# Gated cross-attention plus top-2 expert layer on one core: a reordered front, fixed PSUM banks, work moved between engines, tail blocks with both expert layers

## The chip, the core and the metric

The kernel runs on one core of a Trainium2 chip. The metric is device time in microseconds (us) from launch to end, the median of several runs. Engines are named as in the profile: PE is the matrix engine (PEld its weight loads), DVE the VectorE, ACT the ScalarE, POOL the GpSimd engine, SP the engine that issues most DMAs. All arithmetic is fp32, except some routing matrices of zeros and small whole numbers, which are bf16.

## What is computed

```python
xn  = layernorm(x)                                   # x: 4 x 256 x 256
q, k = ctx @ Wq.T + bq, ctx @ Wk.T + bk              # ctx: 4 x 256 x 128
att = softmax(q @ k.T)                               # 256 x 256 for each of 4 batches
x   = x + tanh(g_xattn) * (xn @ att.T)
t   = layernorm(x)                                   # 1024 rows
probs = softmax(gelu(t @ rw1) @ rw2)                 # 8 experts
w, idx = top_k(probs, 2)
for e in 8 experts, k in 2 choices:                  # I = 1024
    Y = gelu(t @ w1[e] + b1[e]) @ w2[e] + b2[e]      # rows whose k-th choice is e
    C = gelu(b1[e]) @ w2[e] + b2[e]                  # all the other rows, if any row chose e
    out += w[k] * where(idx[k] == e, Y, C)
x = x + tanh(g_ffn) * out
```

The constant C of an expert needs the product of gelu(b1[e]) with w2[e]. A row of an expert's hidden layer has gelu(b1[e]) subtracted, so that the constant can be added to all rows at the end.

## The kernel before

**Front.** Rows are held in 8 tiles of 128 (two for each batch). One string, `order` (L446), lists every step of attention, second layernorm and gating; each step puts its instructions on fixed engines, and every engine works through its own instructions in the order in which the string names them. Step names used below, with the key of a batch or a group of tiles behind a colon: `qk` the two projections on PE (L218), `q` and `k` their evictions with bias (L225, L228), `en` the scores on PE, `nmax` the negated row maximum on DVE (L243), `exp` on ACT, `rden` the reciprocal of the sum (L258), `norm` the scaling (L264: DVE, for batch 3 ACT), `pt` and `attT` transposition and eviction, `st`, `pw`, `xn` the first layernorm (statistics on DVE, power -0.5 on POOL, scaling on DVE, for batch 3 POOL), `tra` and `xnT` its transposition, `po` the product with the attention, `add` the residual on DVE (L350), `sf`, `pf`, `xf` the second layernorm (`xf` also writes the rows to DRAM through SP), `trf`, `xT`, `r`, `gel`, `lg` the gate network, `chosen` (L396) the ranks of the eight logits on DVE, `gb1` the gelu of all b1, `table:F` a one-element activation that loads F's table, `w2:n` n loads of 1 MB of w2 through SP. PSUM tiles come from a pool of eight banks in turn. Batch 3 stays behind: its `po`, `add` and gate are done later.

**Routing.** Rows of the first six tiles (12 groups of 128 row-choices) are sorted into slots of 128 rows, each of one expert (L930): `cnt`, `pc`, `scan`, `over`, `runs`, `past`, `who`, `lead`, `rank`, `pos`, `split`, `put` are small DVE and PE steps, `hq_` (L647) makes a 128x128 one-hot matrix for each group on DVE, `inv_` (L651) multiplies them on PE, and `lists` writes the row numbers. `fill:0` loads w1 of slot 0 through SP as soon as `who` is known; `gather` (L760, POOL) fetches a slot's rows from DRAM.

**Slots.** Each slot has `turn` (L773: two PE transposes of the gathered rows, an ACT copy), `first_layer` (L787: 8 x 2 matmuls `h`, a gelu on ACT for each 128 hidden units, two subtractions on DVE) and `second_layer` (L809: 8 matmuls `y` of 128x256, scaling `ys` on DVE, an indirect DMA from POOL that adds the rows to the output, each after the one before). The fixed loop (L1013) has 16 slots and always runs `first_layer(s)` and then `second_layer(s - 1)`. Two queues of small work, `main` and `second`, are slipped in between the matmuls by a credit in us (`between`, L998). `main` holds what batch 3 still needs (`xf:3`, `r:3`), the sorting of the remaining rows, and then the constants: for each expert eight DVE steps `bias_path` (L838), two `both_`, and at the end one DMA that adds the constants to the output (L888).

**Between routing and slot 1** the order is written out (L930 to L942): `gather:0`, `gather:1`, `table:Gelu`, `turn(0)`, then ACT copies the expert list (`who_later`), on which SP waits before it can load w1 of slot 1; five DMAs `ow` bring the rows x to the output, and `sf:3 pf:3` run ahead of `gather:4` (slots 2 to 4).

**Tail.** How many slots are used is known only at run time: blocks of `tc.If` follow (L1046). A block runs `first_layer(s)` and `second_layer(s - 1)`; when no slot follows, an Else runs the last `second_layer`.

## Time and profile before

| what | value |
|---|---|
| median of 3 runs | 203.71 us (203.51 to 204.03) |
| the profiled execution | 202.87 us |
| its span, first to last instruction | 201.1 us |
| PE busy | 178.9 us (89%), 1198 matmul records |
| DVE, ACT, POOL busy | 134.7, 88.1, 73.1 us |
| slots that ran | 19 (L796 has 608 records, 32 for a slot) |
| one slot in the middle (turn, h, y) | 0.22 + 3.57 + 3.46 = 7.25 us |

An fp32 matmul leaves two records. In the timeline the durations of neighbours on one engine overlap a little, so the distance between two starts is what an instruction occupies. The page's row PEclk is the granted clock of PE, in tenths of full speed; before the first clock record (10.9 us into the span) it says nothing.

### The profile page before, as it was taken

What the parts mean: (1) busy time and instruction counts of PE and PEld (TensorE: products, weight loads), DVE (VectorE), ACT (ScalarE), POOL (GpSimd) and SP (SyncE); (2) the same over time, 40 slices, a digit from 0 to 9 for tenths busy, and PEclk for the clock granted to TensorE, in tenths of its full rate; (3) what the DMA queues carried; (4) which work ended last, traced back from release to release, by engine and by line L of the source; (5) the groups of instructions that cost most, each with busy time, mean ns of one, the idle gap of its engine ahead of it and who ended that gap; (6) DMA issues with size and microseconds to landing.
All of it is one profiled execution on the core that took longest, in us unless ns stands there. A gap on an engine that the chain in (4) does not pass through costs nothing.

```text
span 201.1 us, 3845 instructions
## 1 busy us (share of the span) xinstructions
PE 178.9 (89%) x1198; PEld 159.3 (79%) x1198; DVE 134.7 (67%) x401; ACT 88.1 (44%) x234; POOL 73.1 (36%) x89
## 2 busy tenths in 40 slices
PE   3999885389799999999999999999999999999930
PEld 1677573359599899998999999999899989999820
DVE  2879988875558969889689999999756222222200
ACT  2275455434554262362463364265196255255000
POOL 5314510046107146341614522522535504646130
PEclk9999999756999999999999999999999999999995
DMA  6799969945996994317478668699713493423121
GB/s 182 225 335 351 348 194 293 367 170 154 344 414 267 256 404 107 52 14 221 78 241 246 217 234 256 186 401 332 220 39 52 53 172 42 64 39 51 39 31 21
DMA packets 23688, 38.76 MB, mean 193 GB/s; under 512 B 2440, under 2 KB 17808, under 8 KB 23664
## 3 DMA queue, kind: packets, MB, share of 16 engines
q1 hardware_dynamic: 18208, 32.16, 46.6%
q0 software_dynamic: 4880, 6.17, 17.9%
q8 instruction: 13, 0.21, 0.5%
q10 hardware_dynamic: 576, 0.13, 0.3%
q14 instruction: 11, 0.09, 0.1%
HBM read 33.21 MB, written 5.64 MB: 193 GB/s over the span
## 4 chain that ended last, share of the span: by engine, by line
PE 65%; DMA 14%; DVE 11%; issue 6%; POOL 1%; ACT 1%; SPq 0%; POOLq 0%; ACTq 0%; DVEq 0%
PE h L796 27%; PE y L815 26%; DMA out<-ys,give 8%; DMA xg<-rows,take 3%; PE qk L223 2%; DMA ctx_sb<-in_ctxT 2%; PE po L339 2%; PE xt L780 2%; DVE acc L353 1%; DVE nmax L246 1%; DVE att L272 1%; DVE st_f L292 1%; PE r L381 1%; PE inv L655 1%; POOL out L820 1%
## 5 line engine op out<-in xcount | busy, mean ns | idle before, releaser
L796 PE MATMUL h<-xs,w 128*128 128x128 f32 x608 | 74.1, 279 | 0.5 <-ACT xs L781 0.5
L796 PEld LDWEIGHTS h<-xs,w 128*128 128x128 f32 x608 | 71.4, 195 | 1.0 <-ACT xs L781 0.9
L815 PE MATMUL y<-w_all,hT 128*128 x304 | 69.5, 381 | 0.1
L800 ACT ACTIVATE hT<-h,bsel 128x128 f32<-128x128 f32 x152 | 55.5, 368 | 14.9 <-PE h L796 4.2
L815 PEld LDWEIGHTS y<-w_all,hT 128*128 128x128 f32 x304 | 56.1, 190 | 7.2 <-issue 0.3
L803 DVE TENSOR_TENSOR hT<-hT,gbsel 128x512 f32<-128x512 f32 x38 | 26.2, 690 | 25.1 <-ACT hT L800 25.0
L820 POOL DMA_INDIRECT out<-ys,give x14 | 22.5, 1609 | 54.3 <-DVE ys L818 32.1
L781 ACT COPY xs<-xt 128x256 f32<-128x256 f32 x20 | 7.5, 372 | 61.7 <-PE xt L780 61.7
L765 POOL DMA_INDIRECT xg<-rows,take x23 | 25.0, 1085 | 22.7 <-ACT prob L695 15.0
L842 DVE SCALAR_TENSOR_TENSOR gsum<-w_all,gb,gsum 128x256 f32<-128x256 f32 x56 | 27.1, 483 | 1.5
L818 DVE TENSOR_SCALAR ys<-y,share 128x256 f32<-128x256 f32 x19 | 9.1, 481 | 16.7 <-PE y L815 16.6
L820 POOL DMA_INDIRECT out<-ys,take x5 | 8.5, 1710 | 16.8 <-DVE ys L818 10.3
L780 PE MATMUL xt<-ident,xg 128*128 128x128 f32 x40 | 8.0, 283 | 2.0 <-ACT xT L374 0.9
L780 PEld LDWEIGHTS xt<-ident,xg 128*128 128x128 f32 x40 | 5.4, 144 | 5.3 <-PE po L339 1.2
L339 PE MATMUL po<-attT,xnT 128*128 128x256 f32 x24 | 7.8, 479 | 0.0
L299 POOL TENSOR_TENSOR rstd_a<-rstd_a,halves 128x2 f32<-128x2 f32 x4 | 3.0, 750 | 12.0 <-DVE rden L260 7.0
L280 PE MATMUL pt<-ident,att 128*128 128x128 f32 x16 | 3.2, 327 | 4.2 <-ACT att L268 4.0
L223 PE MATMUL qk<-ctx_sb,wq_sb 128*128 128x256 f32 x6 | 3.5, 686 | 3.8 <-DMA wq_sb<-in_wqT 3.4
L697 POOL TENSOR_TENSOR prob<-euler,prob 128x16 f32<-128x16 f32 x1 | 2.9, 2932 | 10.5 <-DVE capped L586 10.5
L851 DVE SCALAR_TENSOR_TENSOR both<-gsum,act,both 128x256 f32<-128x256 f32 x14 | 6.4, 481 | 0.2
L339 PEld LDWEIGHTS po<-attT,xnT 128*128 128x128 f32 x24 | 5.4, 236 | 1.2 <-ACT attT L285 0.3
L280 PEld LDWEIGHTS pt<-ident,att 128*128 128x128 f32 x16 | 1.9, 156 | 5.5 <-ACT att L268 4.4
(201 smaller groups left out, 172.3 us busy)
## 6 DMA issues: line engine op xcount, KB each, us to landing
w<-in_w SPq DMA_DIRECT2D x18, 1024.0 KB
w_all<-in_w SPq DMA_DIRECT2D x8, 1024.0 KB
acc<-in_x SPq DMA_DIRECT2D x4, 256.0 KB
w<-in_w SPq DMA_DIRECT2D x2, 512.0 KB
out<-acc POOLq DMA_DIRECT2D x1, 1024.0 KB
rows<-xf SPq DMA_DIRECT2D x3, 256.0 KB
out<-acc SPq DMA_DIRECT2D x3, 256.0 KB
ctx_sb<-in_ctxT SPq DMA_DIRECT2D x3, 128.0 KB
```

What stands on the lines that cost most here:

```text
L223: nc.tensor.matmul(dst, lhsT=w, rhs=ctx3 if b == "3" else ctx_sb[:, int(b), :], start=True, stop=True)
L339: nc.tensor.matmul(ps[:, ts(i, N)], lhsT=live["xnT", b][:, n, ts(t % LT, P)], rhs=live["attT", b][:, n, :], start=(n == 0), stop=(n == NN ...
L765: nc.gpsimd.indirect_dma_start(out=xg, out_offset=None, in_=rows[0 : EARLY * P if s < NA else T, :], in_offset=bass.IndirectOffsetOnAxis(a ...
L780: nc.tensor.transpose(ps[:, ts(c, P)], xg[:, ts(c, P)], ident)
L781: nc.scalar.copy(xs, ps[:, 0:D].rearrange("p (c l) -> p c l", c=DC))
L796: nc.tensor.matmul(ps[:, 0:P], lhsT=w1_sb[:, c, ts(ch, P)], rhs=xs[:, c, :], start=(c == 0), stop=(c == DC - 1),)
L800: nc.scalar.activation(hT[:, ch, :], ps[:, 0:P], AF.Gelu, bias=bias[:, ch : ch + 1])
L803: nc.vector.tensor_tensor(hT[:, part, :], hT[:, part, :], gbias[:, part].rearrange("p (i o) -> p i o", o=1).to_broadcast([P, 4, P]), ALU.s ...
L815: nc.tensor.matmul(ps[:, 0:D], lhsT=hT[:, i, :], rhs=w2_sb[:, i, :], start=(i == 0), stop=(i == IC - 1))
L818: nc.vector.tensor_scalar(ys, ps[:, 0:D], go.share[:, j : j + 1], None, ALU.mult)
L820: nc.gpsimd.indirect_dma_start(out=total[0:last_row, :], out_offset=bass.IndirectOffsetOnAxis(ap=go.give[:, j : j + 1], axis=0), in_=ys, i ...
L842: nc.vector.scalar_tensor_tensor(gsums[e], w2_all[:, e, c, :], gb1[:, e, c : c + 1], b2_row[e % 2] if c == 0 else gsums[e], ALU.mult, ALU.add)
```

## The change

- **PSUM**: eight fixed banks, each step's bank written in a table (`bank_of`); the pools of the slot phase open after routing.
- **Loads**: the four context tiles are loaded ahead of the four x tiles. Of w2, five loads as before, two after `xf:2a`, one behind `fill:0`.
- **PE at the start**: seven matmuls of a constant tile (`ahead:7`).
- **Attention by query halves** for batches 0 and 2 (keys x and y). `norm` moves to ACT for batches 1 to 3, `xn` of batch 1 to POOL, the epsilon of both layernorms from DVE to POOL. The gate factor tg moves from `norm` into `add`, which becomes a scalar_tensor_tensor. Tiles 2 and 3 become groups 1a and 1b. Logits of batches 0 and 1 are copied by ACT, and tiles 4 and 5 are ranked together.
- **Routing**: of the 12 one-hot matrices DVE makes 8, POOL 2 (`hqp`), ACT 2 (`hqa`, a Square and a Relu for each); `put` comes behind them, `po:3` behind `inv`.
- **Constants of experts 0 and 1** on PE: 16 matmuls `ce` with one column of gelu(b1) as the stationary operand, placed between routing steps, and two ACT copies `cec`; 14 net `bias_path` steps on DVE fall away.
- `sf:3 pf:3` run before `turn(0)`. The `ow` DMAs are four.
- **Tail**: `second_layer(15)` follows the fixed loop, and each block runs `first_layer(s)` and then `second_layer(s)`; there is no Else. The first three blocks are not nested.

```diff
+    banks = [psum.tile([P, 512], F32, name=f"bank{i}") for i in range(8)]
...
-    load_x(0)
-    nc.sync.dma_start(out=ctx_sb[:, 1, :], in_=ctxT[:, 1, :])
-    load_x(1)
...
+    nc.sync.dma_start(out=ctx_sb[:, 1 : B - 1, :], in_=ctxT[:, 1 : B - 1, :])
     nc.sync.dma_start(out=ctx3, in_=ctxT[:, B - 1, :])
-    load_x(3)
+    for b in range(B):
+        load_x(b)
...
+            if key[0] == "0":
+                nc.vector.tensor_scalar(att[:, i, :], att[:, i, :], scale, None, ALU.mult)
+            else:
+                nc.scalar.activation(att[:, i, :], att[:, i, :], AF.Copy, scale=scale)
...
-        nc.vector.tensor_scalar(rstd, mv[:, :, 1], EPS, None, ALU.add)
...
+        nc.gpsimd.tensor_scalar(rstd, mv[:, :, 1], EPS, None, ALU.add)
         nc.gpsimd.tensor_tensor(rstd, rstd, halves.to_broadcast(list(rstd.shape)), ALU.pow)
...
+        normal("a", b, rows_of(b), made("xn", b, [P, LT, D], 3), nc.gpsimd if b in "13" else nc.vector)
...
+    def ahead_(n):
+        for _ in range(int(n)):
+            nc.tensor.matmul(banks[0][:, 0:P], lhsT=ones, rhs=ones, start=True, stop=True)
+    def ce(i):
+        e, c = divmod(int(i), IC)
+        nc.tensor.matmul(
+            banks[bank_of[f"ce{e}"]][0:1, 0:D], lhsT=gb1[:, e, c : c + 1], rhs=w2_all[:, e, c, :],
+            start=(c == 0), stop=(c == IC - 1),
+        )
+    def cec(e):
+        nc.scalar.copy(sums[0:1, int(e), :], banks[bank_of[f"ce{e}"]][0:1, 0:D])
...
+        ahead:7 table:Tanh g ident w2:5 qk:0 qk:1 k:0 q:0 st:0 en:0y tg en:0x q:1 nmax:0y qk:3 pw:0 k:1 nmax:0x exp:0y
+        st:1 qk:2 k:3 exp:0x en:1 xn:0 pw:1 k:2 rden:0y q:3 rden:0x tra:0 norm:0y xn:1 q:2 nmax:1 en:3 xnT:0 norm:0x
+        masks pt:0y exp:1 st:2 en:2x pt:0x en:2y attT:0y nmax:2x pw:2 tra:1 attT:0x rden:1 st:3 po:0 norm:1 nmax:2y
+        xnT:1 xn:2 pw:3 exp:2x pt:1 nmax:3 exp:2y tra:2 xn:3 rden:2x attT:1 add:0 norm:2x po:1b rden:2y sf:0 norm:2y
+        po:1a add:1b pt:2y sf:1b pt:2x xnT:2 pf:0 tra:3 add:1a attT:2y sf:1a attT:2x pf:1b gb1 po:2b xf:0 pf:1a xf:1b
+        trf:0 xnT:3 add:2b po:2a xf:1a xT:0 sf:2b trf:1b r:0 add:2a pf:2b sf:2a xT:1b trf:1a r:1b xf:2b gel:0 pf:2a
+        xT:1a trf:2b lg:0 gel:1b xf:2a w2:2 xT:2b r:1a lc:0 trf:2a r:2b gel:1a chosen:0 xT:2a lg:1b lg:1a gel:2b r:2a
+        lc:1 ce:0 chosen:1 gel:2a lg:2b table:Exp lg:2a ce:1 chosen:2 ce:2 exp:3 ce:3
...
+        if engine is nc.scalar:
+            far = one([P, P], "far", BF16)
+            nc.scalar.activation(far, rowb, AF.Square, scale=-1.0, bias=at)
+            nc.scalar.activation(dst, far, AF.Relu, scale=-1.0, bias=ones[:, 0:1])
...
+            cnt:0 ce:4 scan pc:0 rden:3 ce:5 over:0 runs:0 norm:3 ce:6 lead:0 past:0 who:0 fill:0 w2:1 ce:7 rank:0 pt:3
+            pos:0 cec:0 ce:8 attT:3 ce:9 split:0 ce:10 hqa hqs hqp ce:11 ce:12 put:0 inv:0 po:3
+        do("lists:0 gather:0 sel:0 soft:0 gather:1")
...
+        do("ce:13 ce:14 ce:15 cec:1 wgt:0 add:3 table:Gelu sf:3 pf:3")
...
-        do("fill:1 ow:0 ow:2a ow:2b ow:1 ow:3 sf:3 pf:3 gather:4")
+        do("fill:1 ow:0 ow:1 ow:2 ow:3 gather:4")
...
+        second_layer(*pending)
...
+        with tc.If(used > s - NA):
...
             turn(s + 1, here[0])
             first_layer(s, here[1])
-            second_layer(*pending)
+            second_layer(s, here[1])
             gather(s + AHEAD)
-        with more_slots.Else():
-            with tc.If(used > s - NA - 1):
-                second_layer(*pending)
```

## The prediction

> **What bounds the kernel now.** I read the page first, its slices by engine.

> ```profile
> PE   3999885389799999999999999999999999999930
> DVE  2879988875558969889689999999756222222200
> PEclk9999999756999999999999999999999999999995
> ```

> A slice is 5.03 us. From slice 12 on PE is full: slots follow each other at 7.25 us, 14 of them without a hole. Nothing that saves DVE, ACT or POOL time can show there. What can move is when the full stretch begins (the front) and how it ends (the tail). In the front DVE is the busy engine, and PE has a hole in slices 7 and 8 that is followed by a reduced clock. The two-microsecond windows say when (columns: start:end, length, busy us and instructions of PE, PEld, DVE, ACT, POOL, granted clock, DMA share, GB/s):

> ```profile
> 36.00:38.00 2.00, 0.00 (x0) 0.00 (x0) 1.86 (x13) 0.49 (x3) 0.00 (x0) 1.00 1.09 366
> 42.00:44.00 2.00, 1.83 (x5) 0.93 (x3) 0.98 (x6) 0.65 (x2) 1.41 (x2) 0.50 0.27 86
> 46.00:48.00 2.00, 2.00 (x12) 2.00 (x11) 1.05 (x8) 0.73 (x2) 1.68 (x2) 0.50 0.29 16
> ```

> PE idles during the sort, then works at half clock from 38 to 48 us; from 42 to 48 the DMAs hardly move anything, because w1 of slot 1 has not been asked for. The chain of waits through this stretch:

> ```profile
> 39.37 0.73 PE inv L655 x24
> 40.10 3.75 PE po L339 x8
> 43.87 0.70 DVE acc L353
> ...
> 46.12 0.72 POOL rstd_f L299
> 46.85 0.19 issue
> 47.04 6.37 DMA xg<-rows,take
> 53.41 0.14 issue
> 53.55 0.41 PE xt L780 x2
> 53.95 1.45 PE h L796 x12
> ```

> So the slow `po:3` delays `add:3`, `sf:3`, `pf:3`; slot 2's gather is queued behind `pf:3` on POOL, its packets run behind w1 of slot 1, and slot 1 can't begin before 53.8. What SP waited for, and the last two scatters:

> ```profile
> SPq L894 <- ACT who_later L938: 9.0, 1, 9.0
> ```

> ```profile
> 190.23 1.56 POOL L820 DMA_INDIRECT out<-ys,give  x1 [4.04 <-DVE ys L818]
> 192.98 0.48 DVE L818 TENSOR_SCALAR ys<-y,share 128x256 f32<-128x256 f32 x1 [3.03 <-PE y L815]
> 194.85 1.55 POOL L820 DMA_INDIRECT out<-ys,give  x1 [3.05 <-DMA out<-ys,give]
> ```

> **A. Attention and gate, up to the last `chosen` (32.56 us before).** The first evictions wait for the bias load and start at 6.36; that load is unchanged, so I start the sum there. DVE's list in the new order, by distances between starts in the timeline: `k:0` 0.48; 14 tiles of statistics at 0.56, 7.9; four half maxima at 0.36 and two whole ones at 0.62, 2.7; five reciprocals 0.5; two half `norm` 0.74; ten tiles scaled by `xn` 0 and 2 and by `xf` at 0.36, 3.6; masks 0.37; `add` 0.70 plus four at 0.44 (0.02 to 0.06 over the tensor_tensor row, as L842's 0.48 stands over 0.42), 2.45; three `chosen` 1.24, 1.24, 1.43. Sum 22.6, end 29.0. Gone from DVE are eight epsilon steps (1.5), four scalings of `norm` (1.5), `xn:1` (0.7), logits copies and one split `chosen` (1.2). PE's list after 6.9 is some 20 us warm, ACT's 17.7: both end earlier, if they don't wait. Waits I find by walking the queues: `xf:2a` waits 0.6 for `pf:2a`, `chosen:0` 0.2 for ACT's copy, and I allow 0.4 for the rest. End 30.2, that is 2.4 earlier; between 1.0 (every edge late) and 3.5 (none).

> The unknown costs here: the epsilon on POOL lies between the small POOL rows (0.13) and the power itself (0.72); I take 0.2, being an add; the four or five on the path cost what the wait above holds. `xn:1` on POOL costs 2.44 (L304, two tiles) against 0.73 on DVE; `tra:1` then waits for it until about 13.4, in a queue with `po:0` behind it, but `po:0` waits for `attT:0x` until 13.9 anyway. The x loads behind the context arrive about 1 us later; DVE is held by the bias until 6.36, so this costs nothing, and up to 0.5 if they come after 6.8. Each fixed bank makes its next writer wait for its last reader; in the walk the tightest are `pt:1` behind `xnT:1` and `pt:2x` behind `add:1b`, both at the moment when their data come: 0, up to 0.3. Gelu's table for `gb1` stands on ACT in front of `xnT:3`, which nothing on DVE waits for in this stretch: 0. `ahead:7` runs where PE waits for weights (until 3.44) and can cost 0.3 at most; if PE is at full clock before 10.9, where its records begin, it is worth up to 2 us to PE, which DVE then hides.

> **B. Sort, from `cnt` to `lists` (32.60 to 40.13, 7.53).** Away: `nmax:3` 0.59, the gate factor 0.24, four of twelve one-hots 0.68. Added: `inv` no longer runs beside the one-hots, since `put` is last: its 0.73 stands open instead of 0.2, +0.5. `rden:3` now waits for `exp:3`, behind the Exp table: +0.2. Two one-hots on POOL: half of L304's 1.22 each, 1.2 to 1.5 in all, beside eight on DVE plus `put` (1.75): covered, unless POOL is held up. [...] By the trace, the power beside DVE's scalings at 8.29 took 0.79, with DVE idle 0.72 and 0.69: 0.1. [...] I take 0.3. The Square and Relu on ACT: four at 0.28 to 0.37, 1.5 at most, covered too. SP's loads of w2 stand behind the row writes and `fill:0`, so w1 of slot 0 has less ahead of it: 0. 7.53 - 1.51 + 0.5 + 0.2 + 0.3 = 7.0; `lists` at 37.3, 2.8 earlier.

> **C. From `lists` to slot 0's first `h` (45.47 before).** `ce`: nearest row `y` L815, 128x256, 0.43 a step (3.46 / 8); a single stationary column may save part of the load (0.3), at half clock it is 0.86. Twelve lie in PE's hole, between `chosen:2` and `put`, 5.2 in 8: no cost, and the longest hole becomes some 1.6 instead of 4.0. So I take the clock as full: `po:3` 1.95 instead of 3.75, ends 39.2; `ce:13` to `15` 1.3, to 40.5; `cec:1` 0.35, 40.9. Then the Gelu table, which sits in front of slot 0's copy `xs`. [...] The gather beside it: `lists` + 0.9 + 1.2 as before, 39.6, and 1.5 for its packets, 41.1: covered. So 2.6 earlier.

> **D. Slot 1 (53.83 before).** The five `ow` DMAs become four, behind w1 of slot 1 as before: 0. PE: `h` of slot 0 at full clock with `trf:3` and `inw` 4.5, two turns 0.8: 48.2. Gather of slot 2: DVE's line after `lists` (selection, first bias, weights 2.8; `add:3`, `sf:3` 1.85) ends at 42, `pf:3` 0.9, gather issued at 43, down by 46 to 48. w1 of slot 1: `who_later` 43.0, issue 0.8 later as before (45.50 to 46.27), and the packets took until 51.6 (1 MB in the windows 48 to 52), 5.3: 49.1. This wait ends last. The 1 MB of w2 queued behind `fill:0` is issued near 33.5; 12 MB at 350 GB/s from 8.9 us (the windows 16 to 24 show 348 to 350) end at 39 to 40, so w1 of slot 1 finds the queue free. Slot 1 begins at 49.3, **4.5 earlier**; between 2.5 and 6.

> **E. Middle.** DVE loses 14 steps of 0.51 and the constants' DMA comes a slot earlier: nothing on PE's path, 0. The b2 loads wait for `both_` on SP, with w1 loads behind them that have two slots (14 us) of room; DVE may wait 2 for b2 of expert 2, as it did once before (2.1 at 101.14) without a hole in PE. If that cover fails, 0.5.

> **F. Tail.** PE's work and its end are the same. But y of the next to last slot is now finished a slot earlier, so the last scatter follows its own `ys` (193.46 + 0.27 = 193.7) instead of the scatter before and two branches (194.85): **1.1 earlier**. `y` of the same slot needs DVE's second subtraction: 1.13 after the last `h` (163.86, 164.99), and its fifth step comes 1.85 after: covered by 0.6. If every `y` waited for the whole hidden tile, three blocks would lose 1.1 each, 3.4.

> **Sum.** 4.5 + 1.1 = 5.6 on a profiled execution of 202.87 (span 201.1 and 1.8 around it): 197.3. The median of the runs is 0.84 higher, so 203.7 - 5.6 = **198.1**.

> **Rivals.**
> 1. *The clock is still lost* in the sort, because matmuls with one stationary column don't keep it up. For: before, `po:3` and `inv` ran from 38.2 to 43.8 without raising it. Against: the clock fell only after 4 us of nothing, and stayed full at 60% busy (22 to 26 us). Then `po:3` 3.75, three `ce` 2.6, table, `xs`: `h` near 46, and half of slot 0 at half clock; slot 1 at 52 to 52.5 with w1. Gain 1.5 + 1.1: 201.1. Chance 0.15.
> 2. *Slower: the clock falls earlier, in the gate network.* Halves and single tiles thin PE's work between 20 and 28 us. If a window there is taken for idle near 24, 4.6 us of PE work become 9.2, `chosen:2` ends at 34, `lists` 41.3, then `po:3` 3.8, `ce` 2.6, table and copies 2.4: `h` at 50.2, w1 of slot 1 0.8 + 5.3 behind `who_later`: slot 1 at 56.5, 2.7 late, minus 1.1: 205.3. It decides once PE is under some 60% over several us ahead of 28. Chance 0.09.
> 3. *The waits between engines eat the front*: A yields nothing, or `y` waits for the whole hidden tile. Gain 2.4 to 3, or about zero with both: 201 to 203.5. Chance 0.13, of which 0.05 within 0.3%.
> 4. *More than forecast*: w1 moves at 350 GB/s in 3 us, PE never waits: slot 1 at 47.5, 196. Chance 0.08. The forecast itself has 0.55.

> A measurement of this kernel tells about 0.3% (0.6 us) from no change. The range 195.8 to 202.0 takes in the forecast, rival 1, rival 4 and half of rival 3.

> **What would show it.** Right: granted clock full from 30 to 50; last `hot` near 30, first gather near 38, first `h` near 43, slot 1's first `h` near 49, and PE without holes after it; the slot still 7.25; the last scatter 0.3 after its `ys`. Wrong: `h` L796 with a mean over 279 ns, holes before `y` in the tail, `inv` waiting for POOL, `xs` waiting for a table.

## The result, and the profile after

| | before | after |
|---|---|---|
| median of the runs | 203.32 us (201.60 to 204.33, 14 runs) | 201.41 us (199.21 to 202.60, 14 runs) |
| the profiled execution | 202.87 us, span 201.1 | 199.21 us, span 197.3 |

The ratio is 0.9898 with a 95% interval of 0.9864 to 0.9932: the changed kernel is about 2.0 us faster. The forecast was 5.6 us. The direction held and the range held; the size was less than half of it. The profiled execution of after is the fastest of its 14, so a second profile of the same kernel (run `r0_after` below: 200.4 us, span 198.6) stands beside it wherever a size is read. Medians and ranges take in every execution; the ratios leave out those over 1.5% above the fastest of their kernel, as the profiled execution of `e5` below was (201.43 us against 198.21), of which no mark is read.

The slices of the page, after:

```profile
PE   7999998849899999999999999999999999999950
DVE  1799879732589979786999999954820230222210
PEclk9999999988999999999999999999999999999995
```

The reader is to see two things. TensorE is busy for 0.8 and more in slices 5 to 8 (counted from 1), where it was down to 0.3 before; and the reduced clock hasn't gone. It has shrunk from slices 8 to 10 to slices 9 and 10, and lies over slot 0 instead of starting in the sort. The two-microsecond windows of after say when (columns as before the change):

```profile
38.00:40.00 2.00, 0.91 (x5) 0.17 (x2) 1.90 (x7) 1.04 (x2) 0.81 (x1) 1.00 1.10 385
40.00:42.00 2.00, 0.41 (x2) 0.20 (x2) 1.35 (x10) 0.81 (x2) 1.29 (x3) 1.00 0.34 118
42.00:44.00 2.00, 1.55 (x7) 1.55 (x8) 0.00 (x0) 0.82 (x3) 1.70 (x2) 0.64 0.23 66
44.00:46.00 2.00, 2.00 (x12) 2.00 (x11) 0.00 (x0) 0.75 (x3) 0.99 (x2) 0.51 0.80 186
```

From 39 to 41.5 TensorE has next to nothing to do, and when slot 0 begins at 42.45 its clock is halved. In the first of these windows the DMAs moved 385 GB/s: the eighth megabyte of w2, which the change put behind `fill:0`. The timeline of `r0_after` shows what stood behind it (in square brackets: idle time of the engine before, and what ended it):

```profile
36.50 1.26 POOL L824 DMA_INDIRECT xg<-rows,take  x1 [1.76 <-DVE lmax L750]
...
41.71 0.66 PE L839 MATMUL xt<-ident,xg 128*128 128x128 f32 x2 [2.57 <-DMA xg<-rows,take]
42.88 5.49 PE L855 MATMUL h<-xs,w 128*128 128x128 f32 x24 [0.51 <-ACT xs L840]
```

The same lines of the kernel before, where TensorE stood for half a microsecond in front of the turn:

```profile
41.20 1.22 POOL L765 DMA_INDIRECT xg<-rows,take  x1 [15.01 <-ACT prob L695]
44.34 0.66 PE L780 MATMUL xt<-ident,xg 128*128 128x128 f32 x2 [0.51 <-PE po L339]
```

Slot 0's rows were asked for at 36.50, 4.7 us earlier than before (41.20), and took 5.1 us to land, where they took 3.0 before; the packets of these rows and of slot 1's ran from 39.7 to 41.4, when those of the load thinned out. In the kernel before the same gather ran while the queues emptied; its packets were through by 43.9, 2.7 us after the request. The 24 matmul records of `h` took 5.49 us; at full clock they take 2.94 (run `e1_w2_late`).

The wait for w1 of slot 1 is what it was (9.0 before):

```profile
SPq L957 <- ACT who_later L1012: 8.9, 1, 8.9
```

The tail did what the forecast said, in the timeline of after:

```profile
190.22 0.48 DVE L877 TENSOR_SCALAR ys<-y,share 128x256 f32<-128x256 f32 x1 [2.36 <-PE y L874]
190.97 1.57 POOL L879 DMA_INDIRECT out<-ys,give  x1 [4.03 <-DVE ys L877]
```

The last scatter starts 0.75 after its `ys`; before, it started 1.87 after it (192.98, 194.85).

The marks of both kernels, in us of the span:

| | before | after | r0_after | forecast |
|---|---|---|---|---|
| last `hot` starts | 32.31 | 28.93 | 29.16 | 30.2 (its end) |
| `lists` (first `take`) | 40.13 | 35.80 | 36.03 | 37.3 |
| first `h` of slot 0 | 45.47 | 42.45 | 42.88 | 42.9 |
| first `h` of slot 1 | 53.83 | 50.69 | 51.93 | 49.3 |
| first `y` | 58.78 | 55.67 | 56.91 | |
| last `y` ends | 192.88 | 190.18 | 191.61 | |
| span ends | 201.1 | 197.3 | 198.6 | |
| half clock before the end | 38.2 to 48.4 | 42.6 to 46.0 | 41.6 to 48.4 | none |

Read from the top: up to `lists` the gain grows to 4.1 to 4.3 us, more than forecast. At slot 0 it is 2.6 to 3.0, at slot 1 1.9 to 3.1. So between `lists` and slot 1 the kernel gave back a quarter to more than half of what it had won. Marks of single profiles are to be read with care: in eleven profiles with this front `lists` lies between 35.8 and 37.1, and in the two with the old front at 40.13 and 39.09 (`b1_tail_alone`). Counted from `lists` the marks hold together: the first `h` of slot 1 comes after 13.7 us before (13.6 in `b1_tail_alone`) and after 14.9 and 15.9 in the two profiles of after, where the forecast had 12.0.

### The profile page after: what moved, and what is told of

Read it like the earlier page. It is cut to its first block, busy times and chain, and to the rows that moved or that the text cites. A ratio compares the mean times of both kernels' runs of the same rounds, so it can differ in the third digit from the quotient of the medians.

```text
span 197.3 us, 3910 instructions
## 1 busy us (share of the span) xinstructions
PE 183.0 (93%) x1248; PEld 162.1 (82%) x1248; DVE 123.0 (62%) x364; ACT 93.0 (47%) x250; POOL 80.2 (41%) x104
## 3 DMA queue, kind: packets, MB, share of 16 engines
q0 software_dynamic: 4880, 6.17, 17.7%
## 4 chain that ended last, share of the span: by engine, by line
PE 46%; DMA 27%; issue 14%; DVE 6%; ACT 2%; POOL 1%; ACTq 1%; POOLq 0%; DVEq 0%
DMA out<-ys,give 20%; PE h L855 19%; PE y L874 14%; DMA out<-acc 5%; PE bank L356 3%; DMA g_sb<-in_gates 2%; PE bank L403 1%; PE bank L248 1%; PE bank L341 1%; PE xt L839 1%; POOL out L879 1%; DVE hqs L708 1%; PE bank L417 1%; PE bank L232 1%; PE bank L291 1%
## 5 line engine op out<-in xcount | busy, mean ns | idle before, releaser
L879 POOL DMA_INDIRECT out<-ys,give x14 | 22.9, 1633 | 52.5 <-DVE ys L877 23.9
L905 DVE SCALAR_TENSOR_TENSOR gsum<-w_all,gb,gsum 128x256 f32<-128x256 f32 x42 | 20.3, 483 | 1.1
L356 PE MATMUL bank<-attT,xnT 128*128 128x256 f32 x32 | 8.0, 388 | 0.3 <-ACT attT L299 0.2
L465 PE MATMUL bank<-w_all,gb 128*1 128x256 f32 x32 | 7.7, 379 | 0.0
L356 PEld LDWEIGHTS bank<-attT,xnT 128*128 128x128 f32 x32 | 5.7, 190 | 1.4 <-ACT attT L299 0.8
L914 DVE SCALAR_TENSOR_TENSOR both<-gsum,act,both 128x256 f32<-128x256 f32 x12 | 5.4, 482 | 0.2
L947 ACT ACTIVATE acc<-sums,wgt 128x256 f32<-128x256 f32 x8 | 3.9, 526 | 2.9 <-DVE sums L941 2.9
L465 PEld LDWEIGHTS bank<-w_all,gb 128*1 128x1 f32 x32 | 2.3, 83 | 3.6 <-issue 0.5
L321 POOL TENSOR_SCALAR xn<-acc,mv_a,rstd_a 128x256 f32<-128x256 f32 x4 | 5.0, 1243 | 0.2
```

The costliest lines, as they stand in the source:

```text
L356: nc.tensor.matmul(ps[:, ts(i, N)], lhsT=live["xnT", b][:, n, ts(t % LT, P)], rhs=live["attT", b][:, n, :], start=(n == 0), stop=(n == NN ...
L465: nc.tensor.matmul(banks[bank_of[f"ce{e}"]][0:1, 0:D], lhsT=gb1[:, e, c : c + 1], rhs=w2_all[:, e, c, :], start=(c == 0), stop=(c == IC - 1),)
L879: nc.gpsimd.indirect_dma_start(out=total[0:last_row, :], out_offset=bass.IndirectOffsetOnAxis(ap=go.give[:, j : j + 1], axis=0), in_=ys, i ...
L905: nc.vector.scalar_tensor_tensor(gsums[e], w2_all[:, e, c, :], gb1[:, e, c : c + 1], b2_row[e % 2] if c == 0 else gsums[e], ALU.mult, ALU.add)
```

## The experiments

All kernels were timed beside the kernel before; a ratio is to the runs of before in the same session, with its 95% interval. The theory that I began with: the changed front made a new hole in front of slot 0, because its rows wait behind the eighth megabyte of w2, and the clock fell in it. The rivals were that ScalarE holds slot 0 anyway, that the clock falls for want of work in the sort (rival 1 of the forecast), and that the tail or the middle took the gain.

### The changed kernel again: r0_after

No edit.

> The changed kernel unaltered, for more profiled executions of it. Theory: the one shown fell to half clock for one clock window (3.4 us) in the hole ahead of slot 0; a typical execution loses more there, so a profile nearer the median of 201.4 should show the reduced clock for two windows (near 7 us) around the first h, or a later start of slot 0, with the middle at 7.25 us a slot and the last scatter unchanged. Rival: what is lost between the profiled execution and the median lies elsewhere (the tail's scatters, or the slots in the middle), and the front is the same. Time: 201 to 202.

Measured: 201.35 us (200.40 to 202.15), ratio 0.9918 (0.9886 to 0.9950). Half clock for 6.83 us, twice as long as in the first profile: slot 0's first 24 records took 5.49 instead of 4.57. One spell of 3.41 us was lost in the first profile and two in this one. That does not explain the 3.4 us between the fastest and the slowest of the 14 executions, though: their times hardly follow their mean granted clock (two at 0.971 took 200.27 and 202.12), so most of that spread has another cause, which stays open. Windows of 3.41 us, cut so that the changes of the clock in this profile fall on their borders:

```profile
34.78:38.19 3.41, 3.10 (x35) 2.35 (x36) 2.32 (x16) 0.48 (x2) 1.39 (x2) 1.00 0.95 335
38.19:41.60 3.41, 0.95 (x5) 0.18 (x3) 3.17 (x16) 1.85 (x3) 1.70 (x3) 1.00 0.86 296
41.60:45.02 3.42, 2.80 (x12) 2.43 (x13) 0.13 (x1) 0.86 (x4) 2.62 (x4) 0.50 0.41 62
45.02:48.43 3.41, 3.41 (x25) 3.35 (x25) 1.33 (x3) 1.47 (x5) 0.51 (x1) 0.50 0.85 267
```

TensorE was busy for 0.95 of 3.41 us, and the next window was granted half the clock; it came back after a window that was busy throughout.

### The eighth megabyte of w2 later: e1_w2_late

```diff
-  ... past:0 who:0 fill:0 w2:1 ce:7 rank:0 pt:3
+  ... past:0 who:0 fill:0 ce:7 rank:0 pt:3
-  do("fill:1 ow:0 ow:1 ow:2 ow:3 gather:4")
+  do("fill:1 w2:1 ow:0 ow:1 ow:2 ow:3 gather:4")
```

> Only the eighth load of w2 is moved from behind w1 of slot 0 to behind w1 of slot 1. Theory (slot 0's rows waited for that megabyte): the first transpose comes at 40 to 40.5 instead of 41.5, the hole in PE shrinks from 2.6 to 1 to 1.5, the clock may stay full; slot 1 starts 1 to 3 us earlier; time 198.5 to 200.5. Rival (the hole is set by ScalarE: constants' copy, Gelu table, then the copy of slot 0's rows): the transposes come earlier but h does not start before 41.2, gain at most 1.2. Rival (DMA order is of no matter): 201.4.

Measured: 198.96 us (198.25 to 200.30), ratio 0.9795 (0.9757 to 0.9833). The timeline of TensorE:

```profile
40.82 0.41 PE L839 MATMUL xt<-ident,xg 128*128 128x128 f32 x2 [0.57 <-DMA xg<-rows,take]
42.48 2.94 PE L855 MATMUL h<-xs,w 128*128 128x128 f32 x24 [1.25 <-ACT xs L840]
49.11 1.60 PE L855 MATMUL h<-xs,w 128*128 128x128 f32 x12
59.53 2.69 PE L855 MATMUL h<-xs,w 128*128 128x128 f32 x22 [1.33 <-DMA w<-in_w]
```

From `lists` (37.14 in this profile) to the first turn it is 3.7 us instead of 5.7, and in this profile the clock stays full up to the end of the work (two of the six executions have a lower mean granted clock, 0.980 and 0.981 instead of 0.991 to 0.994, and took 200.30 and 198.78). To slot 0's first `h` it is 5.3 us instead of 6.7 and 6.9, and no less, since its copy `xs` now waits for the Gelu table (until 41.96): that rival was right about the next limit. Slot 1 begins at 49.11, 12.0 us after `lists`, as the forecast had it. But the weights of slot 2 now lie behind the megabyte, and slot 2 waits for them. Still 2.4 us under the changed kernel.

### Work for TensorE in the hole: e2_fill and e3_both

`e2_fill` puts twelve products of ones into the hole; `e3_both` does this and moves the megabyte as well. Their products are not used.

```diff
-  do("ce:13 ce:14 ce:15 cec:1 wgt:0 add:3 table:Gelu sf:3 pf:3")
+  do("ce:13 ce:14 ce:15 ahead:12 cec:1 wgt:0 add:3 table:Gelu sf:3 pf:3")
```

> Only twelve matmuls of the constant tile are added on TensorE in the hole between the last constant matmul and slot 0's transposes (2.6 us at full clock); nothing else moves, and their result is used by nothing. Theory (what was lost is the clock): granted clock full from 30 us to slot 1, h of slot 0 shorter by 1.7 to 3.4 us, slot 1 at 48.7 to 49.5 with w1's landing as the next wait; time 198 to 199.7, and less spread between executions. Rival (the clock fell for another reason, or it is not on the path): no change, 201.4, or 0.3 slower if the fillers are in the way of the transposes.

> Both: the late w2 load and the twelve fillers. Theory: the gains don't add fully, since slot 1 then waits for w1 of slot 1, whose load is issued after slot 0's copy; slot 0 starts at 41.5, slot 1 at 48 to 48.7; time 197 to 199. Rival: same as the better of the two alone.

Measured: `e2_fill` 201.53 us (198.82 to 203.37), ratio 0.9873 (0.9813 to 0.9934); `e3_both` 199.60 us (198.96 to 202.49), ratio 0.9839 (0.9789 to 0.9889). In `e2_fill` slot 0 ran at full clock, but began later (44.11), slot 1 waited for its weights until 51.21, and the clock fell in that hole (51.4 to 54.9). Both miss what I expected (198 to 199.7, 197 to 199). So keeping the clock up in one hole was mostly worth nothing while the transfers were late: the next hole took it. The one execution of `e2_fill` with a mean granted clock of 0.989 took 198.82, the others (0.980 to 0.986) 201.26 and more. In `e3_both` the clock did not fall before the end, but the products themselves stood in the way: they ran from 39.97 to 42.9, and the turn, whose rows had landed by 40.4, came behind them at 43.02. Neither beats `e1_w2_late`.

### Without the constants on TensorE: e6_no_constants_on_PE

All `ce` and `cec` are taken out, and VectorE makes these constants in the middle, as before.

```diff
-        if e < 2:
-            gsums[e] = b2_row[e]
-            nc.vector.tensor_tensor(b2_row[e][0:1, :], b2_row[e][0:1, :], sums[0:1, e, :], ALU.add)
-            return
...
-            main += [f(.47, bias_path, e, c) for c in range(IC if e > 1 else 1)]
+            main += [f(.47, bias_path, e, c) for c in range(IC)]
```

> Changed kernel without the two constants on TensorE: their 16 groups of one-column matmuls and the two copies are gone, and VectorE makes them in the middle, as in the kernel before. If they held the clock through the sort, as the prediction had it: half clock from about 35 to 45 and over slot 0, as before; ScalarE has no copy to wait for, so the first h of slot 0 at 41.5 to 42, but slowed, slot 1 at 51 to 52; time 201 to 202.5. If the clock does not hang on them: half clock no longer than the changed kernel's and a time of 199.5 to 200.5, since slot 0 starts earlier without them.

Measured: 201.92 us (200.81 to 202.77), ratio 0.9934 (0.9902 to 0.9966). Windows of this kernel:

```profile
29.00:32.00 3.00, 1.28 (x6) 0.82 (x5) 2.72 (x16) 1.82 (x7) 0.00 (x0) 0.50 1.07 356
32.00:35.00 3.00, 0.00 (x0) 0.00 (x0) 2.86 (x17) 2.08 (x5) 1.35 (x2) 0.50 0.93 284
35.00:39.00 4.00, 3.88 (x32) 3.23 (x32) 2.60 (x16) 1.84 (x4) 2.14 (x2) 0.50 0.95 313
42.60:46.00 3.40, 2.49 (x10) 2.12 (x11) 0.04 (x1) 0.83 (x3) 2.60 (x4) 0.51 0.21 47
```

Without the constants TensorE has a hole in the sort and works at half clock from 29.0 to 39.2, as the kernel before did from 38.2 on. With them it doesn't: in after the granted clock is 1.00 from 28.90 to 42.55. So here the matmuls with one stationary column held the clock through the sort, and rival 1 of the forecast falls; the constants took away the old hole, and the clock then fell in the next one, which this kernel has too (42.6 to 49.5). In time the two kernels lie within their intervals of each other, so what the constants are worth here isn't measured.

### The order of weights, rows and table

These six kernels all move the megabyte behind the weights of slot 1; they differ in three things: where the weights of slot 2 (`fill:2`) go, whether the Gelu table comes ahead of the last constant, and whether slot 2's rows are asked for ahead of `pf:3`. `e1_w2_late` has none of the three.

```diff
 e4, e5  do("fill:1 w2:1 fill:2 ow:0 ow:1 ow:2 ow:3 gather:4")
 e7 on   do("fill:1 w2:1 ow:0 ow:1 ow:2 ow:3 fill:2 gather:4")
 e4, e8  do("table:Gelu ce:13 ce:14 ce:15 cec:1 wgt:0 add:3 sf:3 pf:3")
 e10     do("ce:13 ce:14 ce:15 cec:1 wgt:0 add:3 table:Gelu sf:3 gather:2 pf:3")
 e11     do("table:Gelu ce:13 ce:14 ce:15 cec:1 wgt:0 add:3 sf:3 gather:2 pf:3")
```

> Changed kernel, with the eighth MB of w2 issued after the weights of slot 1 and ahead of the weights of slot 2, which themselves now go ahead of the writes of total; and with the Gelu table loaded before the last constant instead of behind its copy. Theory (the first slots wait for transfers and for the table, one after the other): no wait of slot 2 on its weights (with the eighth MB moved alone it was 2.2 us), first xs some 0.7 us earlier than 42.07, first h of slot 0 at 41.8, of slot 1 at 48.4, no half clock before the end; time 197.0 (196 to 198), 2 us under the 198.96 of the first move alone. Rival (from slot 2 on TensorE is held by something else, so that what the start gains is paid back): slot 2 earlier, but the last y no earlier than 190.0 and the time 198.5 to 199.5.

> As the last, but with the Gelu table where the changed kernel has it (behind the second constant's copy). Theory: the wait of slot 2 is gone, slot 0 and 1 stay at 42.5 and 49.1, time 197.7 (197 to 198.5); so 0.7 us of the last run's gain belongs to the table and 1.3 to the order of the weights. Rival: 198.5 to 199.5, as with the eighth MB moved alone.

> Changed kernel with the eighth MB of w2 behind the weights of slot 1 (as in the run that gave 198.96) and the weights of slot 2 behind the writes of total and ahead of the rows of xf:3. Theory (the rows of slots 1 and 2 have to stay ahead of the megabytes, the weights of slot 2 have to come before 57): slot 1 at 49.1, slot 2 without its 2.2 us wait, rows of slot 2 in time, no half clock in most executions; time 197.7 (197 to 198.5). Rival (what the start gains is paid back later whatever the order): 198.5 to 199.5, no better than 198.96.

> The last with the Gelu table loaded ahead of the last constant. Theory: xs 0.7 us earlier than with the table behind the copy, first h of slot 0 at 41.6 to 41.8; slot 1 no earlier than its weights (asked for when slot 0's xs is copied, 0.8 + 5.5 later, 48.5 at the earliest), so 0.3 to 0.6 us less than the last run. Rival (slot 0 is held elsewhere): no difference between the two, within 0.3 us.

> The run with the weights of slot 2 behind the writes of total (199.1), and the gather of slot 2 asked for ahead of the power of the last block on GpSimd, so about 1.2 us earlier (41.2 to 41.4 instead of 42.5) and in any case ahead of the weights of slot 1 (42.7). Theory (rows that are asked for after two megabytes arrive behind them, at 47 to 48 instead of 43): rows of slot 2 down by 43.5; slot 1 was not held by them here, so slot 0 and 1 as before, within 0.4, and 198.6 to 199.3. Rival (the rows' place does nothing to the time here or in the next run).

> The last with the Gelu table ahead of the last constant. With the gather of slot 2 behind the megabytes this had cost 2.5 us (201.62 against 199.1). Theory (it cost only because the weights of slot 1 then were asked for at 41.93, before the rows of slot 2 at 42.48, and the rows landed 1.5 us later, held slot 1 until 50.3, and the clock fell): with the rows first, slot 0 at 41.1, slot 1 at 48.1 to 48.6, no half clock in most executions, time 198.0 to 198.8. Rival (the early table itself, or an earlier slot 0, costs the time): slot 1 at 50 or later again and 201 to 202.

| kernel | `fill:2` | table | rows of slot 2 | median, us | ratio (95%) | slot 0, slot 1 in the profile |
|---|---|---|---|---|---|---|
| e1 | later | behind | behind `pf:3` | 198.96 | 0.9795 (0.9757 to 0.9833) | 42.48, 49.11 |
| e5 | ahead of `ow` | behind | behind `pf:3` | 199.54 | 0.9802 (0.9748 to 0.9857) | not read |
| e4 | ahead of `ow` | ahead | behind `pf:3` | 200.98 | 0.9875 (0.9821 to 0.9929) | 41.10, 49.92 |
| e7 | behind `ow` | behind | behind `pf:3` | 199.10 | 0.9783 (0.9761 to 0.9804) | 41.94, 48.89 |
| e8 | behind `ow` | ahead | behind `pf:3` | 201.62 | 0.9906 (0.9880 to 0.9932) | 41.12, 50.31 |
| e10 | behind `ow` | behind | ahead | 199.38 | 0.9769 (0.9725 to 0.9814) | 41.62, 49.75 |
| e11 | behind `ow` | ahead | ahead | **196.62** | 0.9669 (0.9628 to 0.9710) | 40.33, 46.93 |

The order of the weights alone (e5, e7) brought nothing over `e1_w2_late`, against the 1.3 us that I expected: slot 2 waits 0.6 us for them in e7 instead of 1.3, and that is all.

The early table was the surprise: I expected 0.3 to 0.6 us from it (e8); it starts slot 0 0.8 us earlier, and it cost 2.5 us (e8 against e7). The timeline of e8, in the order of the starts:

```profile
41.93 0.37 SPq L138 DMA_DIRECT2D w<-in_w  x1
42.35 0.47 SPq L129 DMA_DIRECT2D w_all<-in_w  x1
42.48 1.09 POOL L824 DMA_INDIRECT xg<-rows,take  x1 [0.19 <-issue]
...
50.06 0.41 PE L839 MATMUL xt<-ident,xg 128*128 128x128 f32 x2 [1.92 <-DMA xg<-rows,take]
...
50.31 2.09 PE L855 MATMUL h<-xs,w 128*128 128x128 f32 x12
```

Since slot 0's `xs` and with it `who_later` come earlier, the megabytes for slot 1 and for w2 are now asked for 0.55 and 0.13 us before slot 2's rows. Those rows then came down between 47.1 and 49.5, behind the first megabyte and over half of the second. In e7 the rows were asked for at 42.51, a quarter of a microsecond before the first megabyte (42.75); they came behind that one all the same, but ahead of the second, and were down by 47.9. The turn of slot 2 stands ahead of slot 1's `h` in TensorE's queue, so slot 1 waits for rows that it doesn't need, and the clock falls behind this hole (51.05 to 54.46). `e4_all_three` has the same order (41.91 and 42.40), and loses too (200.98 against 199.54 of e5, with intervals that overlap). `e11_rows_table` tells that from a fault of the early table itself: with the rows asked for first, the same table makes a gain of 2.8 us against e10, more than I expected (198.0 to 198.8 for e11). Its timeline:

```profile
39.10 0.95 POOL L824 DMA_INDIRECT xg<-rows,take  x1 [0.30 <-issue]
...
40.33 2.94 PE L855 MATMUL h<-xs,w 128*128 128x128 f32 x24 [0.51 <-ACT xs L840]
...
41.13 0.37 SPq L138 DMA_DIRECT2D w<-in_w  x1
...
46.93 1.60 PE L855 MATMUL h<-xs,w 128*128 128x128 f32 x12
```

No half clock until the last slot is done (mean granted clock 0.989 to 0.993 in its five executions, 0.971 to 0.987 in 14 of the changed kernel), slot 1 at 46.93, and a time 3.3% under the kernel before and 2.3% under the changed kernel (by the two ratios, 0.9669 / 0.9898). Part of that 2.8 is the clock: in the profile of e10 the 1.3 us in which `xs` waits for the table were enough to lose it for 3.41 us (TensorE busy 1.59 of the 3.41 before), in e11 it was kept (2.40 of 3.41). The executions of e10 tell what that is worth: two with a mean granted clock of 0.988 and 0.989 took 198.28 and 197.66, four at 0.979 and 0.980 took 199.33 to 199.61. So some 1.4 of the 2.8 us are the clock, an estimate from the distance of those two to the median.

### The tail alone, the old tail, and the start

`b1_tail_alone` is the kernel before with the changed blocks of the tail; `b2_old_tail` the changed kernel with the old ones; `e9_no_ahead` the changed kernel without `ahead:7`. The edits are the tail part of the diff, forward and back, and one word of `order`.

> Kernel before with the changed tail alone (each block holds both layers of one slot). By the tail step of the prediction 1.1 us less: time 202.0, ratio 0.9945, first slots exactly as before, and from the end of the last y to the end of the span some 7.2 instead of 8.2. Rival (the tail's gain comes from the shift of the front): ratio within 0.2% of 1.

> Changed kernel with the old tail (the last slots' second layer in a block of its own behind a branch). By the prediction's tail step 1.1 us more than the changed kernel: 202.5, with 8.2 instead of 7.1 from the last y to the end. From the run with the tail alone (ratio 0.9994), in which 1.1 us at the end were saved and 0.8 us went into a hole of TensorE at 164: 0 to 0.6 us more, 201.4 to 202.0, and the hole smaller than with the new tail.

> Changed kernel without the seven products of ones at the start of TensorE. Theory (they lift the clock from about 5 us on, where it would otherwise rise at 8 to 11): the first projections and energies at half clock, 0.3 us longer each for some 8 of them; the last hot 0.5 to 1.5 us later, everything behind it as much, time 0.5 to 1.5 above the changed kernel's 201.4. Rival (the front follows VectorE, which waits for DMAs at first): last hot within 0.3 and the time within 0.4 of the changed kernel's.

Measured: `b1_tail_alone` 202.72 us, ratio 0.9994 (0.9962 to 1.0026); `b2_old_tail` 202.59 us, ratio 0.9952 (0.9922 to 0.9982), which is 0.3 to 0.5% above the changed kernel (0.7 to 1.1 us), with intervals that just overlap. Both profiles show the step that was forecast: the last scatter starts 0.76 after its `ys` in `b1_tail_alone`, and `b2_old_tail` needs 8.65 from the last `y` to the end where the changed kernel needs 7.1. With the old front, though, the time doesn't show it. Two things in that profile take some of it back. From the start of the last scatter to the end of the span it has 7.1 us, where before, after, `r0_after` and `b2_old_tail` have 6.2 to 6.4. And there is a hole of TensorE in front of a `y`:

```profile
165.15 7.17 PE L815 MATMUL y<-w_all,hT 128*128 x32 [0.76 <-issue]
```

Such a hole, once in a run, is in nearly all kernels with a changed part: 0.42 in after, 0.72 in `r0_after`, 0.77 in `b2_old_tail`, 0.22 in `e11_rows_table`; before had 0.11 at 163.86. As `b2_old_tail` has it too, the new tail isn't its cause. Nothing in the profile is seen to release it; its cause stays open.

`e9_no_ahead`: 202.31 us, ratio 0.9945 (0.9912 to 0.9978), 0.3 to 0.5% above the changed kernel, inside the intervals. Its last `hot` starts at 29.41, inside the 28.9 to 30.3 of the profiles with the products, as the rival had it; its time lies where the theory had it. Whether the seven products are worth anything isn't settled.

## Why the prediction was right in sign and wrong in size

- **A (attention and gate)** held: in eleven profiles with this front the last `hot` ended between 29.2 and 30.5, against 30.2. The two of the changed kernel (29.2 and 29.4) are among the earliest, so what they gained beyond the forecast is not the change's. From VectorE's first `k` to that end it is 23.1 to 24.1 us, which leaves 0.5 to 1.5 of waits beside the list's 22.6, where I allowed 1.2. The first `k` started between 5.7 and 6.8; the sum began at 6.36.
- **B (sort)** held: 6.6 us from the end of `hot` to `lists`, against 7.0. The 0.3 for GpSimd held up by VectorE is shown by no run: GpSimd's two one-hots took 0.68 us each beside VectorE's, and ended a tenth before VectorE's own eight; ScalarE's took 0.40 each instead of the 0.28 to 0.37 that I took, and ended just ahead of `inv`.
- **C (up to slot 0)** gave the right number, 42.9 (45.47 less 2.6), by a wrong way. The 2.0 us from its 40.9 on hold Gelu's table and the copy `xs`; in the traces the load took 1.28, the next activation began 1.30 after the load's start before (41.16, 42.46) and 1.29 in after (39.33, 40.62), and `xs` took 0.37. `lists` was 1.3 to 1.5 us earlier than forecast, and slot 0 was not: that the two cancel is luck. The first step that failed is the gather beside it, "39.6, and 1.5 for its packets, 41.1: covered". (The 39.6 takes 1.1 from `lists` to the request, as the trace has it; with the 0.9 that is written it would be 39.4.) Its request came at 36.5 rather than 38.4, but the packets ran behind the megabyte that I had written off in B with "w1 of slot 0 has less ahead of it: 0". From request to landing it was 5.1 us instead of some 2.7, and from `lists` to slot 0's first `h` 6.7 and 6.9 instead of 5.6; with that load out of the way it is 5.3 (`e1_w2_late`). D even gave a time at which the load would end, 39 to 40. Its sum doesn't come out (12 MB at 350 GB/s are 34 us, from 8.9 on that is 43); it came near because 1.8 of the 12 MB had gone before 8.9, and the load ended at 40.7. I asked what it does to weights, never what it does to rows, although I had read in the kernel before that slot 2's rows ran behind w1.
- **C again: "So I take the clock as full".** This is the step that cost the forecast most of its size. I tested the clock against the old hole in the sort (rightly: `e6_no_constants_on_PE`) and took it as settled. But my own times left TensorE without work from the end of the last constant (40.5) to slot 0's first `h` (42.9), the turn's 0.4 apart: two microseconds that I didn't test. There the clock fell. Slot 0's first 24 records of `h` took 4.57 to 5.49 instead of 2.94, that is 1.6 to 2.6 us.
- **D (slot 1)**: from slot 0's first `h` to slot 1's I forecast 6.4, with w1 of slot 1 as the wait that ends last. It wasn't: in after, `r0_after`, `e1_w2_late` and `e11_rows_table` TensorE doesn't wait for it, and its own chain ends last (`h`, `trf:3`, 0.9 us for ScalarE's `xT`, two turns). At full clock that chain takes 6.6 (`e1_w2_late`, `e11_rows_table`) where I had 5.3, so the 6.4 was near by luck; with the clock lost it takes 8.2 to 9.1. From `lists` to slot 1 the forecast's 12.0 thus became 14.9 and 15.9: 1.1 and 1.3 of it by the late rows, 1.8 and 2.6 by the clock. So 4.5 became 1.9 to 3.1.
- **E (middle)**: I forecast 0. From the first to the last `y` it was 0.4 to 0.6 us more than before (134.5 and 134.7 against 134.1), of which the hole in front of one `y` holds most (0.42 and 0.72 against 0.11).
- **F (tail)**: 1.1 forecast. From the start of `ys` to that of the scatter it is 1.87 before and 0.75 after, 1.1. In the time this isn't shown: `b1_tail_alone` gained nothing (0.9994), and the interval of `b2_old_tail` overlaps that of the changed kernel.

The sum for `r0_after`, whose time is near the median: 1.9 (slot 1) + 1.2 (last `y` to the end, 8.2 to 7.0) - 0.6 (the middle) = 2.5, the difference of the two spans (201.1 - 198.6). The medians differ by 1.9. That the megabyte ahead of slot 0's rows, and the hole that it made, are the cause is shown: with the load moved alone (`e1_w2_late`) slot 1 starts 12.0 us after `lists`, as forecast, and 2.4 us come back; with the next two obstacles gone (`e11_rows_table`) the kernel is at 196.6, below the forecast. How much of the 2.4 us is the clock and how much the rows isn't separated, since this edit mends both. Within `e2_fill`, `e4_all_three` and `e10_rows_first` the executions with the highest clock were faster than all the others, by 1.0 to 2.4 us; in `e1_w2_late` and `e7_w1_after_total` those with the lower clock were not slower on the whole. Rival 1 named the right loss, a clock at half speed over slot 0, and a near time (201.1), but gave a cause that `e6_no_constants_on_PE` excludes.

## What to carry to other kernels

When a stage is made earlier, walk every queue again up to the next full stretch: a row gather that used to find idle queues may now stand behind a bulk load (here 5.1 us from request to landing instead of 3.0), and a load issued half a microsecond sooner may slip in front of rows that are needed first (0.55 us ahead of them in `e8_w1_table`, slot 1 at 50.31; 0.24 us behind them in `e7_w1_after_total`, slot 1 at 48.89). Ask for the small, urgent transfers before the large ones, even if they are needed later than the issuing engine's other work (ratio 0.9669 in `e11_rows_table`, 0.9906 in `e8_w1_table`). And where TensorE's clock is at stake, test each remaining hole of the new schedule, not only the one that the change fills.
